# Three row tiles for every expert, and ten looked-up slots for the fourth ones

## The chip, the cores and the metric

The kernel runs on one core of one Trainium2 chip. The metric is the device time of one execution in microseconds (us), and it is compared by the median of several runs. One profiled execution gives the trace: for each engine, when every instruction started, how long it took and what ended the wait in front of it. TensorE (PE) multiplies, VectorE (DVE) and ScalarE (ACT) work element by element, GpSimd (POOL) does small work and starts indirect DMAs, and SyncE (SP) starts ordinary DMAs; ACT starts some too.

## The reference

x has 3125 rows of 256 numbers. Four blocks follow each other, each added to x after a layer norm: three layers of graph attention, a mixture of 16 experts, a sum over graph neighbours, and a mixture of 8 experts. The change touches the second block, which computes, for every row:

```python
probs = softmax(x @ gate_w + gate_b)                 # 16 experts
top_probs, top_idx = top_k(probs, 2)                 # each row goes to two experts
top_probs = top_probs / sum(top_probs)
hidden = silu(x @ w1[e]) * (x @ w2[e])               # 256 -> 512, for each expert e
out = sum over the two experts of  top_prob * (hidden @ w3[e])    # 512 -> 256
```

All of it is in f32. For the inputs that are timed, the 6250 pairs of row and expert spread over the experts as 473, 306, 378, 384, 428, 407, 354, 351, 470, 372, 338, 459, 390, 379, 405 and 356 rows.

## The kernel before

The kernel works on 25 tiles of 128 rows. While the third attention layer is still multiplying, a router handles its output in groups of two tiles (class `Router`): it forms the gate's logits, takes the two best experts of each row, counts with small matmuls how many rows each expert has so far, and writes each normalised row, with its number and its weight, by an indirect DMA into a list in memory, `rows0`. Each expert owns a stretch of 3200 places there (NP), and its rows stand at the beginning of its stretch. An earlier step (`spare_rows`, L1411) has filled the first 512 places (CAP0) of every stretch with spare rows, whose number points behind the real rows and whose weight is zero. The router's last step, `finish` (L660), takes the largest of the sixteen counts. If it is above 512, the flag sends the whole computation to a slower general path at the end (L1516 to L1522); otherwise that path is skipped.

`routed_experts` (L667) then multiplies. For each expert it loads w1, w2 and w3 (512 KB each, ACT's queue, L682 to L686, two buffers), and the first 512 rows of the list as four tiles (`xs`, SP's queue, L688). VectorE copies the rows' numbers to integers (`who`, L690). TensorE transposes the rows (L695) and ScalarE copies them out (L696). For each of the four column blocks of the hidden layer, TensorE forms two products of 128 x 512 (p1 and p2, L703), ScalarE takes silu of the one (L706), and VectorE multiplies it with the other (`hid`, L707). Then, for each of the four row tiles, TensorE multiplies back to 256 columns (L711), VectorE scales by the row's weight (`y`, L714), and POOL starts an indirect DMA that adds the 128 rows of y into `sums` in memory (L716). The accumulates of one expert are independent of each other, since its rows are of different tokens (`independent`, L542); those of the next expert may hold the same tokens and wait for the last expert's to have landed. At the end, five loads bring `sums` back as the new x (L720), and the third block starts from them.

The order on each engine is set by a scheduler that takes program order and available buffers into account: it moves loads and the copy of `who` ahead, so that `who` of the next expert stands in VectorE's queue before the `hid` products of this one. Buffers are recycled: a tile of a pool with two buffers waits until all that used the tile before the last one is done, and for `who` that includes the accumulates which read it.

The last block, `routed_top1` (L723), already works with slots: a table of expert and place for each slot is made on the chip, and SP and TensorE read it into registers (L867, L869) to load rows by a computed address.

Of the kernel before, what the change touches and what calls it, by code (L numbers as in the profile page):

```python
# [9 lines left out]
F32 = mybir.dt.float32  # L10
F16 = mybir.dt.float16
BF16 = mybir.dt.bfloat16
I32 = mybir.dt.int32
U8 = mybir.dt.uint8
F32R = mybir.dt.float32r
AF = mybir.ActivationFunctionType
OP = mybir.AluOpType
AX = mybir.AxisListType
# [3 lines left out]
P = 128  # L22
N = 3125
NT = 25
LAST = N - (NT - 1) * P
NP = NT * P
D = 256
# [492 lines left out]
CAP0 = 512  # L520
CAP1 = 1024
# [26 lines left out]
class Router:  # L548
# [6 lines left out]
    def __init__(self, tc, cp, ident, eps, iota, count, rows, sums, gate_w, gate_b):  # L555
        nc = self.nc = tc.nc
        self.tc, self.ident, self.eps, self.iota, self.rows, self.sums = tc, ident, eps, iota, rows, sums
# [102 lines left out]
    def finish(self, pp, over):  # L660

        total = pp.tile([1, NX0], F32, name="ps_z")
        self.nc.tensor.matmul(total, self.every[:, 0:1], self.pre[:, NT], start=True, stop=True)
        self.nc.vector.tensor_reduce(over, total, AX.X, OP.max)


def routed_experts(tc, x, ident, rows, sums, w1, w2, w3):  # L667
# [6 lines left out]
    nq = CAP0 // P  # L674
    with tc.tile_pool(name="rw", bufs=2) as ep, tc.tile_pool(name="rx", bufs=2) as xp, \
         tc.tile_pool(name="rs", bufs=3) as sp, \
# [3 lines left out]
        for e in range(NX0):  # L680
# [7 lines left out]
            nc.sync.dma_start(xs, rows[e * NP:e * NP + CAP0].rearrange("(q p) f -> p q f", p=P))  # L688
            who = xp.tile([P, nq], I32, name="who")
            nc.vector.tensor_copy(who, xs[:, :, D])  # L690
            xsT = xp.tile([P, KD, CAP0], F32, name="xsT")
            for k in range(KD):
                ps = tp.tile([P, CAP0], F32, name="ps_x")
                for q in range(nq):
                    nc.tensor.transpose(ps[:, q * P:(q + 1) * P], xs[:, q, k * P:(k + 1) * P], ident)  # L695
                nc.scalar.copy(xsT[:, k], ps)  # L696
            hid = xp.tile([P, nh, CAP0], F32, name="hid")
            for j in range(nh):
                p1 = pp.tile([P, CAP0], F32, name="ps_h1")
                p2 = pp.tile([P, CAP0], F32, name="ps_h2")  # L700
                for ps, w in ((p1, a), (p2, b)):
                    for k in range(KD):
                        nc.tensor.matmul(ps, w[:, k, j * P:(j + 1) * P], xsT[:, k], start=(k == 0),  # L703
                                         stop=(k == KD - 1))
                s = sp.tile([P, CAP0], F32, name="silu")
                nc.scalar.activation(s, p1, AF.Silu)  # L706
                nc.vector.tensor_tensor(hid[:, j], s, p2, op=OP.mult)  # L707
            for q in range(nq):
                ps = po.tile([P, D], F32, name="ps_o")
                for j in range(nh):  # L710
                    nc.tensor.matmul(ps, hid[:, j, q * P:(q + 1) * P], o[:, j], start=(j == 0),  # L711
                                     stop=(j == nh - 1))
                y = sp.tile([P, D], F32, name="y")
# [4 lines left out]
                    in_=y, in_offset=None, bounds_check=NP + CAP0 - 1, oob_is_err=True, compute_op=OP.add))  # L718
        for t in range(0, NT, 5):
            nc.sync.dma_start(x[:, t:t + 5], sums[t * P:(t + 5) * P].rearrange("(t p) f -> p t f", p=P))  # L720
# [236 lines left out]
def dense_attention(tc, dram, counts, x_in, big, ident, eps, layers, src, dst, rows, high, make_router, over):  # L957
# [10 lines left out]
    with tc.tile_pool(name="dw", bufs=1) as cp, tc.tile_pool(name="dwl", bufs=2) as wl, \  # L968
# [9 lines left out]
        with tc.tile_pool(name="dp", bufs=8) as pmp, tc.tile_pool(name="ds", bufs=2) as sp, \  # L978
# [148 lines left out]
            router.finish(zp, over)  # L1127
# [283 lines left out]
def spare_rows(tc, cp, rows0, rows1):  # L1411
# [16 lines left out]
    to.append((rows1[NX1 * NP:], empty1))  # L1428
    return [lambda o=o, i=i: nc.scalar.dma_start(o, i) for o, i in to], [empty0[:, 0, 0:1], empty1[:, 0:1]]
# [3 lines left out]
def routed(ctx: ExitStack, tc: tile.TileContext, i: dict, out: bass.AP, over):  # L1433
# [5 lines left out]
    rows0 = dram.tile([NX0 * NP, ROW0], F32, name="rows0")  # L1439
# [4 lines left out]
    early = ctx.enter_context(tc.tile_pool(name="early", bufs=1))  # L1444
    with tc.tile_pool(name="counts", bufs=1) as kp:
# [3 lines left out]
                                                            i["L0_ffn_gate_w"], i["L0_ffn_gate_b"]), over[:, 0:1])  # L1449
        with tc.tile_pool(name="s0", bufs=1) as sp:  # L1450
            ws, wm = (two_halves(nc, sp, i["L1_gnn_" + n], "s_" + n) for n in "WM")
            hidden = hidden_weights(nc, early, *(i["L1_ffn_" + n] for n in ("W1", "b1", "Wg", "bg")), x[:, 0, 0:1])
            routed_experts(tc, x, ident, rows0, sums, *(i["L0_ffn_" + n] for n in ("w1", "w2", "w3")))
# [95 lines left out]
```

## Time and profile before

| quantity | value |
|---|---|
| median of 3 runs | 2082.47 us (2082.14 to 2083.78) |
| the profiled execution's own time | 2082.07 us |
| its span, first to last instruction | 2080.4 us |
| TensorE busy over the span | 1915.8 us, 92% |
| mean granted TensorE clock | 0.982 |
| VectorE, ScalarE, POOL busy | 1010.3, 740.7, 289.3 us |
| attention products (L1075), busy | 864.3 us |
| expert products p1 and p2 (L703), busy | 225.0 us |
| expert output products (L711), busy | 113.1 us |
| accumulates into sums (L716), on POOL | 64, 1552 ns each |
| loads of w1, w2, w3 | 48 of 512 KB, 4.2 us median to landing |
| loads of xs | 16 of 516 KB, 5.8 us median to landing |

The page divides the span into 40 slices of 52 us and gives each engine's busy share in tenths; the experts lie in slices 23 to 29, from 1189.7 us (the first transposes) to 1548.7 us (the last accumulate landed). A group's line gives line, engine, operation, output and inputs, shapes and count, then total busy time, mean duration in ns, and the idle time before it with what ended it. Ends of matmuls are modelled, so durations of single matmuls overlap; rates are better read from start to start. PEld is the load of weights into TensorE.

### The profile page before, as it was taken

How to read it: one execution, taken by the hardware profiler on the slowest of the kernel's cores; microseconds unless marked ns; L12 is line 12 of the kernel's file. 1: busy time of each engine (PE TensorE's matmuls, PEld its weight loads, DVE VectorE, ACT ScalarE, POOL GpSimd, SP SyncE). 2: the span in 40 equal slices, each digit the busy share in tenths (PEclk: the TensorE clock that was granted, in tenths of full speed). 3: DMA queues.
4: the chain of work that ended last, by engine and by line, in shares of the span. 5: the costliest groups of instructions: out<-in, count | busy, mean ns of one | idle time of the engine just before them, and what ended most of it. 6: DMA issues, size and time to landing. Idle time of an engine off the chain costs nothing. (4 is left out here: it accounts for less than half of the span.)

```text
span 2080.4 us, 27180 instructions
## 1 busy us (share of the span) xinstructions
PE 1915.8 (92%) x9234; PEld 1466.8 (71%) x9234; DVE 1010.3 (49%) x2897; ACT 740.7 (36%) x2224; POOL 289.3 (14%) x394
## 2 busy tenths in 40 slices
PE   2999998789999999999999699999979999997986
PEld 2788886668788888788888356556547887555775
DVE  5888886767455544477777422122225222232211
ACT  2866754556010000121111211111116998443221
POOL 1200000000000000023332222323220000222211
PEclk9999999999999999999999799999989999998999
DMA  4002146550000000011111344545530000624553
GB/s 123 25 1 83 42 170 277 203 203 24 3 1 1 0 1 3 8 54 52 49 42 37 122 101 124 130 102 126 127 84 1 1 1 23 240 102 173 190 181 114
DMA packets 97344, 173.82 MB, mean 84 GB/s; under 512 B 9718, under 2 KB 70485, under 8 KB 97168
## 3 DMA queue, kind: packets, MB, share of 16 engines
q10 hardware_dynamic: 37906, 78.75, 10.8%
q1 hardware_dynamic: 42028, 57.91, 8.9%
q0 software_dynamic: 17264, 35.33, 6.5%
q8 instruction: 76, 1.25, 0.2%
q14 instruction: 70, 0.57, 0.1%
HBM read 82.98 MB, written 91.35 MB: 84 GB/s over the span
## 5 line engine op out<-in xcount | busy, mean ns | idle before, releaser
L1075 PE MATMUL acc<-big,pm 128*128 128x257 f32 (+1 forms) x3750 | 864.3, 383 | 2.3 <-DVE pm L1072 2.0
L1075 PEld LDWEIGHTS acc<-big,pm 128*128 128x128 f32 (+1 forms) x3750 | 688.5, 188 | 112.7 <-DVE pm L1072 6.7
L1072 DVE SCALAR_TENSOR_TENSOR pm<-tau,rho,counts 128x256 f32<-128x256 f32 (+1 forms) x975 | 427.0, 467 | 151.7 <-PE acc L1075 150.2
L703 PE MATMUL ps_h<-xsT,w 128*128 128x512 f32 x512 | 225.0, 597 | 3.6 <-ACT xsT L696 3.6
L703 PEld LDWEIGHTS ps_h<-xsT,w 128*128 128x128 f32 x512 | 96.4, 191 | 122.8 <-issue 110.5
L1404 PE MATMUL acc_c<-ohk,ohs 128*128 128x200 f16 x1176 | 135.0, 254 | 31.6 <-ACT ohs L1389 19.7
L1392 DVE TENSOR_TENSOR ohk<-iota_k,key 128x1200 f16<-128x1200 f16 x196 | 151.2, 776 | 20.2 <-PE acc_c L1404 19.4
L1193 PE MATMUL acc<-msg,cr 128*128 128x512 f32 (+1 forms) x625 | 158.0, 405 | 0.1
L1404 PEld LDWEIGHTS <-ohs 128*128 128x128 f16 x1176 | 102.8, 99 | 62.1 <-ACT ohs L1389 32.3
L1407 ACT CAST counts<-acc_c 128x400 uint8<-128x400 f32 x196 | 95.4, 489 | 135.7 <-PE acc_c L1404 131.2
L1189 ACT ACTIVATE cr<-counts 128x256 fp32r<-128x256 uint8 (+1 forms) x325 | 130.6, 402 | 22.0 <-DMA sums<-y,who 13.0
L716 POOL DMA_INDIRECT sums<-y,who x64 | 99.3, 1552 | 265.6 <-DVE y L714 250.9
L1193 PEld LDWEIGHTS acc<-msg,cr 128*128 128x128 f32 (+1 forms) x625 | 115.1, 186 | 28.8 <-ACT cr L1189 1.2
L1388 ACT ACTIVATE far<-iota_s,low 128x128 f16<-128x128 f16 x360 | 124.6, 404 | 4.7 <-issue 2.2
L855 PE MATMUL ps_y<-t_wd,hsT 128*128 x512 | 116.9, 382 | 0.0
L711 PE MATMUL ps_o<-w,hid 128*128 128x256 f32 x512 | 113.1, 379 | 0.0
L711 PEld LDWEIGHTS ps_o<-w,hid 128*128 128x128 f32 x512 | 97.3, 190 | 20.1 <-issue 7.7
L855 PEld LDWEIGHTS ps_y<-t_wd,hsT 128*128 128x128 f32 x512 | 95.5, 192 | 12.0 <-ACT hsT L882 0.3
L706 ACT ACTIVATE silu<-ps_h 128x512 f32<-128x512 f32 x64 | 38.2, 597 | 161.0 <-PE ps_h L703 161.0
L707 DVE TENSOR_TENSOR hid<-silu,ps_h 128x512 f32<-128x512 f32 x64 | 43.7, 687 | 106.4 <-PE ps_h L703 106.3
L764 PE MATMUL ps_H<-big,t_w 128*128 128x512 f32 (+1 forms) x224 | 93.1, 552 | 0.7 <-ACT H L766 0.5
L1094 DVE TENSOR_SCALAR col<-acc 128x2 f32<-128x2 f32 (+1 forms) x39 | 6.1, 156 | 161.1 <-PE acc L1075 161.1
(240 smaller groups left out, 1777.8 us busy)
## 6 DMA issues: line engine op xcount, KB each, us to landing
rows<-empty ACTq DMA_DIRECT2D x16, 2564.0 KB, 8.8
w<-in_L_ffn_w_dram ACTq DMA_DIRECT2D x48, 512.0 KB, 4.2
hs<-rows SPq DMA_DIRECT2D x32, 641.0 KB, 4.1
rows<-empty ACTq DMA_DIRECT2D x16, 516.0 KB, 3.7
xs<-rows SPq DMA_DIRECT2D x16, 516.0 KB, 5.8
t_wd<-in_L_ffn_Wd_dram SPq DMA_DIRECT2D x8, 1024.0 KB, 10.4
bias<-in_L_ffn_bd_dram SPq DMA_DIRECT2D x32, 128.0 KB, 4.0
big<-sums SPq DMA_DIRECT2D x5, 640.0 KB, 8.5
```

Of the source, the lines that this page charges most:

```text
L703: nc.tensor.matmul(ps, w[:, k, j * P:(j + 1) * P], xsT[:, k], start=(k == 0), stop=(k == KD - 1))
L711: nc.tensor.matmul(ps, hid[:, j, q * P:(q + 1) * P], o[:, j], start=(j == 0), stop=(j == nh - 1))
L716: independent(tc, f"sums{e}", nc.gpsimd.indirect_dma_start(out=sums[:, :], out_offset=bass.IndirectOffsetOnAxis(ap=who[:, q:q + 1], axis=0 ...
L855: nc.tensor.matmul(ps, hsT[:, j], d[:, ds(e, 1), j, :].rearrange("p o f -> p (o f)"), start=(j == 0), stop=(j == nh - 1))
L1072: nc.vector.scalar_tensor_tensor(pm[:, :n], tau[:, :n], now.rho[:, s:s + 1], edges[:, s, :n], op0=OP.max, op1=OP.mult)
L1075: nc.tensor.matmul(acc[:r, j, :D + 1], pm[:, q:q + r], now.h[:, s], start=(s == 0), stop=(s == NT - 1))
L1189: nc.scalar.activation(cr[:, :n], edges[:, s, :n], AF.Copy, accum_out=seen[:, a * NT + s:a * NT + s + 1])
L1193: nc.tensor.matmul(acc[:r, j].rearrange("p h d -> p (h d)"), cr[:, q:q + r], msg[:, s].rearrange("p h d -> p (h d)"), start=(s == 0), stop ...
L1388: nc.scalar.activation(far[:, i], self.iota_s, AF.Abs, scale=-1.0, bias=self.low32[:, pair, i:i + 1])
L1392: nc.vector.tensor_tensor(to[:, i:].rearrange("p t (x u) -> p t x u", u=2), iota.rearrange("p (x u) -> p x u", u=2)[:, None].to_broadcast( ...
L1404: nc.tensor.matmul(acc[:, u], ohs[:, i], ohk[:, i], start=(t == 0), stop=(t == TW - 1))
L1407: nc.scalar.copy(to[:, :, d0 % PAIR:d0 % PAIR + 2 * WIN].rearrange("p s (u d) -> p u s d", u=2), acc.rearrange("p u (s d) -> p u s d", d=WIN))
```

## The change

Every expert now multiplies three tiles (EACH = 3), so 384 rows. For experts with more than 384 rows, ten slots (MORE = 10) follow, each of one tile. `finish` makes the table of slots on the chip: it compares each count with 384, forms running sums over the experts, and finds for each slot which expert is its, and so where the fourth tile begins. Slots that are left over take the last expert's weights and a spare tile behind the lists, which `spare_rows` now fills too. If more than ten experts have a fourth tile, the flag is set that sends the work to the general path.

In a slot, SP reads the expert and the place into registers and loads the tile and the three weights by computed addresses. TensorE transposes two blocks, forms p1 and p2 as 16 products of 128 columns into one bank each, ScalarE and VectorE take silu and product in two halves, TensorE multiplies back with four products, VectorE scales, and POOL starts one accumulate, which is a group of its own. The weights' pool has three buffers instead of two, silu's two instead of three, and y has a pool of three.

```diff
+EACH = 3
+MORE = 10
...
-    def finish(self, pp, over):
-
+    def finish(self, cp, pp, over):
+        nc = self.nc
         total = pp.tile([1, NX0], F32, name="ps_z")
+        nc.tensor.matmul(total, self.every[:, 0:1], self.pre[:, NT], start=True, stop=True)
+        nc.vector.tensor_reduce(over, total, AX.X, OP.max)
+        end = cp.tile([1, 5, 2 * NX0], F32, name="more_end")
+        nc.vector.memset(end, 0.0)
+        nc.vector.tensor_scalar(end[:, 0, NX0:], total, float(EACH * P), None, op0=OP.is_gt)
+        for j in range(4):
+            nc.vector.tensor_tensor(end[:, j + 1, NX0:], end[:, j, NX0:], end[:, j, NX0 - (1 << j):-(1 << j)],
+                                    op=OP.add)
+        end = end[:, 4, NX0:]
+        much = cp.tile([1, 1], F32, name="more_much")
+        nc.vector.tensor_scalar(much, end[:, NX0 - 1:], float(MORE), float(2 * CAP0), op0=OP.is_gt, op1=OP.mult)
+        nc.vector.tensor_tensor(over, over, much, op=OP.max)
+        slot = cp.tile([1, MORE], F32, name="more_slot")
+        nc.gpsimd.iota(slot, pattern=[[1, MORE]], base=0, channel_multiplier=0, allow_small_or_imprecise_dtypes=True)
+        done = cp.tile([1, MORE, NX0], F32, name="more_done")
+        nc.vector.tensor_tensor(done, end[:, None, :].to_broadcast([1, MORE, NX0]),
+                                slot[:, :, None].to_broadcast([1, MORE, NX0]), op=OP.is_le)
+        nc.vector.tensor_reduce(slot, done, AX.X, OP.add)
+        table = self.table
+        nc.vector.tensor_scalar(table[:, 0], slot, float(NX0 - 1), None, op0=OP.min)
+        nc.vector.tensor_scalar(slot, slot, float(NP), float(EACH * P), op0=OP.mult, op1=OP.add)
+        nc.vector.tensor_scalar(table[:, 1], slot, float(NX0 * NP), None, op0=OP.min)
...
-    nq = CAP0 // P
-    with tc.tile_pool(name="rw", bufs=2) as ep, tc.tile_pool(name="rx", bufs=2) as xp, \
-         tc.tile_pool(name="rs", bufs=3) as sp, \
+    nq = EACH
+    with tc.tile_pool(name="rw", bufs=3) as ep, tc.tile_pool(name="rx", bufs=2) as xp, \
+         tc.tile_pool(name="rs", bufs=2) as sp, tc.tile_pool(name="ry", bufs=3) as yp, \
...
-            nc.sync.dma_start(xs, rows[e * NP:e * NP + CAP0].rearrange("(q p) f -> p q f", p=P))
+            nc.sync.dma_start(xs, rows[e * NP:e * NP + EACH * P].rearrange("(q p) f -> p q f", p=P))
...
+        for slot in range(MORE):
+            e = nc.values_load(table[0:1, 0, slot:slot + 1], engines=(mybir.EngineType.SP,), min_val=0,
+                               max_val=NX0 - 1, skip_runtime_bounds_check_because="min with the last expert")
+            at = nc.values_load(table[0:1, 1, slot:slot + 1], engines=(mybir.EngineType.SP,), min_val=0,
+                                max_val=NX0 * NP, skip_runtime_bounds_check_because="min with the spare tile")
+            xs = xp.tile([P, ROW0], F32, name="xs")
+            nc.sync.dma_start(xs, rows[ds(at, P)])
+            a = ep.tile([P, KD, HID0], F32, name="w1")
+            nc.sync.dma_start(a, w1[ds(e, 1)].rearrange("o (k p) h -> p (o k) h", p=P))
+            b = ep.tile([P, KD, HID0], F32, name="w2")
+            nc.sync.dma_start(b, w2[ds(e, 1)].rearrange("o (k p) h -> p (o k) h", p=P))
+            o = ep.tile([P, nh, D], F32, name="w3")
+            nc.sync.dma_start(o, w3[ds(e, 1)].rearrange("o (k p) f -> p (o k) f", p=P))
+            who = xp.tile([P, 1], I32, name="who")
+            nc.vector.tensor_copy(who, xs[:, D:D + 1])
+            xsT = xp.tile([P, KD, P], F32, name="xsT")
+            ps = tp.tile([P, KD, P], F32, name="ps_x")
+            for k in range(KD):
+                nc.tensor.transpose(ps[:, k], xs[:, k * P:(k + 1) * P], ident)
+            nc.scalar.copy(xsT, ps)
+            p1 = pp.tile([P, nh, P], F32, name="ps_h1")
+            p2 = pp.tile([P, nh, P], F32, name="ps_h2")
+            for ps, w in ((p1, a), (p2, b)):
+                for j in range(nh):
+                    for k in range(KD):
+                        nc.tensor.matmul(ps[:, j], w[:, k, j * P:(j + 1) * P], xsT[:, k], start=(k == 0),
+                                         stop=(k == KD - 1))
+            hid = xp.tile([P, nh, P], F32, name="hid")
+            for j in range(0, nh, 2):
+                s = sp.tile([P, 2, P], F32, name="silu")
+                nc.scalar.activation(s, p1[:, j:j + 2], AF.Silu)
+                nc.vector.tensor_tensor(hid[:, j:j + 2], s, p2[:, j:j + 2], op=OP.mult)
+            ps = po.tile([P, D], F32, name="ps_o")
+            for j in range(nh):
+                nc.tensor.matmul(ps, hid[:, j], o[:, j], start=(j == 0), stop=(j == nh - 1))
+            y = yp.tile([P, D], F32, name="y")
+            nc.vector.tensor_scalar(y, ps, xs[:, D + 1:D + 2], None, op0=OP.mult)
+            independent(tc, f"more{slot}", nc.gpsimd.indirect_dma_start(
+                out=sums[:, :], out_offset=bass.IndirectOffsetOnAxis(ap=who, axis=0), in_=y, in_offset=None,
+                bounds_check=NP + CAP0 - 1, oob_is_err=True, compute_op=OP.add))
...
+    to.append((rows0[NX0 * NP:], empty0[:, 0]))
...
-    rows0 = dram.tile([NX0 * NP, ROW0], F32, name="rows0")
+    rows0 = dram.tile([NX0 * NP + P, ROW0], F32, name="rows0")
...
+    more = early.tile([1, 2, MORE], I32, name="more")
```

In the expert loop every CAP0 in a tile's width becomes EACH * P, and `y` comes from its own pool.

## The prediction

> **What bounds the kernel now.** I read the page's slices first, then the groups, the waits of the expert stage (1190 to 1549 us) and one expert's timeline.
>
> ```profile
> PE   2999998789999999999999699999979999997986
> PEclk9999999999999999999999799999989999998999
> ...
> L703 PE MATMUL ps_h<-xsT,w 128*128 128x512 f32 x512 | 225.0, 597 | 3.6 <-ACT xsT L696 3.6
> ...
> L711 PE MATMUL ps_o<-w,hid 128*128 128x256 f32 x512 | 113.1, 379 | 0.0
> ```
> TensorE is 9 tenths busy at full clock through the slices of the expert stage (23 to 29), so its passes set the pace there. An f32 matmul is two passes, hence x512 for 256 matmuls. One expert as a timeline (start, length, engine):
>
> ```profile
> 1492.67 7.07 PE L711 MATMUL ps_o<-w,hid 128*128 128x256 f32 x32
> ...
> 1499.07 1.55 POOL L716 DMA_INDIRECT sums<-y,who  x1 [0.30 <-issue]
> ...
> 1499.58 1.04 PE L695 MATMUL ps_x<-ident,xs 128*128 128x128 f32 x8
> 1499.78 0.38 ACTq L686 DMA_DIRECT2D w<-in_L_ffn_w_dram  x1
> 1499.78 0.48 DVE L714 TENSOR_SCALAR y<-ps_o,xs 128x256 f32<-128x256 f32 x1 [1.25 <-PE ps_o L711]
> ...
> 1500.29 0.36 SPq L688 DMA_DIRECT2D xs<-rows  x1
> 1500.85 14.00 PE L703 MATMUL ps_h<-xsT,w 128*128 128x512 f32 x32 [0.24 <-ACT xsT L696]
> 1500.92 1.55 POOL L716 DMA_INDIRECT sums<-y,who  x1 [0.30 <-issue]
> ...
> 1506.76 0.17 DVE L690 CAST who<-xs 128x4 int32<-128x4 f32 x1 [6.50 <-DMA sums<-y,who]
> 1506.87 0.69 DVE L707 TENSOR_TENSOR hid<-silu,ps_h 128x512 f32<-128x512 f32 x1
> ...
> 1514.69 1.67 PE L711 MATMUL ps_o<-w,hid 128*128 128x256 f32 x7
> ```
> The cycle is 22.02 us (L703 starts at 1500.85, one expert before at 1478.83): 13.84 for the 32 passes of L703 (to the start of L711, 1478.83 to 1492.67), 6.91 for the 32 passes of L711 (1492.67 to 1499.58), 1.27 for eight transposes and the first copy (1499.58 to 1500.85). T below is 1499.58, where an expert's last output matmul ends. Beside this runs a second chain that hides: the four accumulates leave POOL 1.86 apart, the last at T+1.34, and VectorE's copy of `who` (L690), which belongs to the next expert, waits until that last one has landed, with the `hid` product queued behind it.
>
> ```profile
> DVE who L690 <- DMA sums<-y,who: 96.1, 14, 8.0
> ```
> Columns: total, times, longest. Nobody waits for VectorE in turn, since TensorE needs that p2 bank back only at T+9.9 (1.27 + 5 x 1.73). How long a landing takes depends on its company (issues of one accumulate each, start in us):
>
> ```profile
> L716 POOL DMA_INDIRECT sums<-y,who x1: 1551/1551/1551, 1499.1 to 1499.1; - x1
> ...
> DMA to landing us min/median/max: 5.8/5.8/5.8
> ```
> ```profile
> L716 POOL DMA_INDIRECT sums<-y,who x1: 1551/1551/1551, 1545.0 to 1545.0; - x1
> ...
> DMA to landing us min/median/max: 3.7/3.7/3.7
> ```
> 5.8 us while w3 (issued at 1499.78) and xs (1500.29) come in, 3.7 us at the end, when nothing is being loaded. The fourth of this group took 5.8 too; over fourteen groups, from the last accumulate's start to `who`, the mean is 6.16, 5.76 to 7.3.
>
> **Experts with three tiles: -88.2 us.** Passes cost by their columns: 0.4325 us at 512 (13.84/32), 0.216 at 256, so 0.324 at 384. L703 becomes 10.38, L711 loses a quarter of its passes, 5.18, transposes and copy 0.95: 16.51 instead of 22.02. Sixteen times 5.51 is 88.2.
>
> **The copy of `who` now bites: +7.** In the changed kernel as built it still stands ahead of the first `hid` product. The last accumulate leaves at T+1.2 (three at POOL's spacing); the gap to `who` I take as 5.8 (6.16 less 0.37, the missing 129 KB of xs at 350 GB/s); `who` to the end of the product was 0.80, now 0.63; to TensorE 0.24: T+7.87. TensorE wants that p2 bank back for its third column block, after 0.95 + 5 x 1.30 = T+7.43. So 0.44 us, fifteen times (experts 1 to 14 and slot 0's copy): 7. Ends: 0 with a gap of 3.7, 29 with 7.3 (1.94 each).
>
> **Ten slots: +90.2.** TensorE alone: a 128-column pass is (1.16-0.28)/7 = 0.126 us in
>
> ```profile
> 1892.31 1.16 PE L764 MATMUL ps_H<-big,t_w 128*128 128x128 f32 x8
> ```
> so 32 passes 4.0 (4.3 with their tail), two transposes 0.3, eight passes of L711's size 1.72: 6.2 per slot. But every slot is its own group, and in the built order the copy of `who` for slot s+1 stands before slot s's `hid` products. It reuses the buffer that slot s-1's accumulate reads, so slot s cannot form `hid`, nor run its output matmuls, before that accumulate has landed. From end of y to end of y: POOL 0.28, start to `who` 5.84 (as 1500.92 to 1506.76), `who` and a 256-column product 0.53, to TensorE 0.24, output matmuls 1.72, to y 0.21, y 0.48: 9.30. The first is 0.26 longer, eight are 9.30, the tenth has no copy behind it and takes TensorE's 6.2: 90.2. The landing is the unknown: loads in company at these offsets (w1 0.7 us after the accumulate's start, w2 1.2) resemble the 5.8 row (w3 0.7 after, xs 1.2 after), which I take. Ends 3.7 (-18.9 in nine periods) and 7.2, the longest of the page's 64 (+12.6).
>
> [...]
>
> **What hides in a slot.** SP: two register loads and four DMAs per slot, behind the wait for y of slot s-1. xs leaves 0.13 later, the weights by about 2.6 (0.83 between SP issues in the last stage, register loads included). 1.65 MB at
>
> ```profile
> 1780.00:1784.00 4.00, 4.00 (x31) 2.70 (x24) 2.58 (x11) 0.59 (x1) 0.00 (x0) 1.00 1.10 350
> ```
> 350 GB/s (last column) is 4.7 us, so all land by about 8.5 after y(s-1); w1 is needed 0.7 us before y(s), at 8.6, the others later. Hidden by little: loads 1 us later than this and paced the same would be met by w1 alone, 1 us a slot. xs, 2.3 us for 128 KB, is there in time for its transposes. big<-sums, queued behind them on SP, waits for the last accumulate anyway.
>
> **The ends: +1.7.** `finish` puts about twelve one-partition VectorE operations at 0.15 to 0.35 us among the last router group's; ten lie ahead of the last g_wt, which POOL's last two row sends wait for, and the first xs waits for these: +2.1 (ends 0 and 3). The third weight buffer loads 1.5 MB more in that idle stretch, behind the other two: 0, at worst 2. The single extra fill joins 33 on ACT's queue in the first attention layer, and POOL's iota an idle POOL: 0; if their cover went, under 1 us together. At the far end the last accumulate starts 0.28 after y instead of 0.66: -0.4. Small reorderings in the early stages: 0, plus or minus 3. POOL's six accumulates fewer and the shorter silu and `hid` operations were not on the path: 0.
>
> **Sum.** -88.2 + 7 + 90.2 + 1.7 = +10.7. The profiled execution took 2082.07 (span 2080.4), 0.4 under the median 2082.47: 2082.47 + 10.7 = 2093.
>
> **Rivals.**
> *The accumulates land early.* For it: 3.7 in the last group, and the slot's own xs is only 129 KB. Against: an accumulate that starts 0.7 us before a load already took 5.8. At 3.7 the slots cost 71.3 and the sum is -8.2: 2074, faster. It turns at a landing of 4.6 (10.7/9 below 5.8), and it is faster beyond 0.2% below about 4.15.
>
> *The clock drops in the slots.* TensorE idles 9.3 - 6.2 = 3.1 us a slot. The granted clock after the stage's end (the last three columns are clock, DMA share, GB/s):
>
> ```profile
> 1546.00:1548.00 2.00, 0.00 (x0) 0.00 (x0) 0.00 (x0) 0.00 (x0) 0.51 (x1) 1.00 0.67 87
> 1548.00:1550.00 2.00, 0.00 (x0) 0.00 (x0) 0.06 (x1) 1.21 (x6) 0.00 (x0) 0.65 0.23 26
> ```
> The last matmul ended near 1543.8; full clock held to about 1548.8, 5 us, then half. A 3.1 us gap is shorter, which speaks against it; its recurring speaks for it. At half clock the output matmuls take 3.45, and nine slots 15.5 more: 2108. [...]
>
> *It doesn't do what it says.* More than ten experts above 384 rows would send everything to the general path, whose time no row shows. From the reference's inputs seven are above 384, the most 473: under 1 in 100. Three slots then multiply the spare tile at full price.
>
> **How the numbers follow.** My forecast (landing 4.9 to 6.5, clock full, 2085 to 2105) 0.50; clock 0.20; early landings 0.17; the rest, longer stalls or late weights, 0.13, mostly above 2100. Early landing reaches down to 2070 with the experts' stall gone as well (-7 more would be 2067, left out); the clock with 7.2 landings reaches 2121 (2093 + 15.5 + 12.6). Range 2070 to 2120. What a measurement here can tell from no change is 0.2%, 4.2 us: faster (below 2078.3) 0.17, same 0.14, slower 0.69.
>
> **What would show it.** Expert cycles of 16.5 to 17.5 us; VectorE's `who` waiting for sums DMAs in nine slots, with TensorE idle before the output matmuls; y to y near 9.3; the clock in the slots; the first xs about 2 us later. The forecast is wrong if slot accumulates land under 4.6 us, if the pace is set by a weight load, or if the clock falls.

## The result, and the profile after

The changed kernel takes 2114.1 us (median of four runs, 2108.7 to 2119.0), the kernel before 2082.6 us beside it: a ratio of 1.0147, with a 95% interval of 1.0126 to 1.0168. It is 31.5 us slower, where 10.7 us had been forecast. The direction and the range held (2070 to 2120), the size did not.

Two rows of the page of the changed kernel, its 40 slices with TensorE's busy share and granted clock in tenths:

```profile
PE   2999998789999999999999599998659999997986
PEclk9999999999999999999999799999779999999999
```

The slots run from 1464 to 1578 us, which is slices 27 (its last third) to 29. TensorE falls from 9 tenths to 8, 6 and 5 there, and the clock to 7 in two slices. In the kernel before, the clock showed 8 in one slice there, after the last expert.

One slot of the changed kernel as a timeline (start, length, engine, line, operation, and in brackets the idle time before it with what ended it):

```profile
1486.53 4.10 PE L772 MATMUL ps_h<-xsT,w 128*128 128x128 f32 x32
...
1486.77 0.48 DVE L783 TENSOR_SCALAR y<-ps_o,xs 128x256 f32<-128x256 f32 x1 [3.10 <-PE ps_o L781]
1487.29 0.35 SPq L753 DMA_DIRECT2D xs<-rows  x1
1487.54 1.55 POOL L784 DMA_INDIRECT sums<-y,who  x1 [9.91 <-DVE y L783]
1488.13 0.37 SPq L755 DMA_DIRECT2D w<-in_L_ffn_w_dram  x1
1488.73 0.37 SPq L757 DMA_DIRECT2D w<-in_L_ffn_w_dram  x1
...
1489.68 0.38 SPq L759 DMA_DIRECT2D w<-in_L_ffn_w_dram  x1
...
1493.82 0.15 DVE L761 CAST who<-xs 128x1 int32<-128x1 f32 x1 [6.56 <-DMA sums<-y,who]
1493.92 0.75 DVE L778 TENSOR_TENSOR hid<-silu,ps_h 128x256 f32<-128x256 f32 x2
...
1494.40 3.52 PE L781 MATMUL ps_o<-w,hid 128*128 128x256 f32 x8 [3.55 <-DVE hid L778]
...
1497.96 0.48 DVE L783 TENSOR_SCALAR y<-ps_o,xs 128x256 f32<-128x256 f32 x1 [3.29 <-PE ps_o L781]
```

The chain is the one forecast: the accumulate starts 0.29 us after y ends, the copy of `who` (L761) waits for it to land, the `hid` product stands behind that copy on VectorE, and the eight passes of the output matmuls wait for `hid`. Two lengths differ. From the accumulate's start to `who` it takes 6.28 us here, forecast 5.84. And the eight passes are shown with 3.52 us, after a gap of 3.55 us in which TensorE had nothing to do. Over the ten slots, the instructions of the accumulate's line and its time to landing:

```profile
L784 POOL DMA_INDIRECT sums<-y,who x10: 1549/1549/1549, 1476.1 to 1578.6; - x10
...
DMA to landing us min/median/max: 3.5/6.6/8.5
```

The output matmuls of the slots, and the clock in two microseconds of them (the last three columns are granted clock, DMA share, GB/s):

```profile
L781 PE MATMUL ps_o<-w,hid x80: 379/634/794, 1472.5 to 1577.4; 128*128 128x256 f32 x80
```

```profile
1484.00:1486.00 2.00, 2.00 (x6) 1.64 (x5) 0.00 (x0) 0.00 (x0) 0.00 (x0) 0.50 0.00 0
```

A median of 634 ns for a pass that takes 379 ns in the experts, and a clock of 0.50. The waits (total, times, longest):

```profile
DVE who L761 <- DMA sums<-y,who: 72.4, 10, 8.8
...
PE ps_o L781 <- DVE hid L778: 36.5, 10, 5.1
```

The first is the copy of `who`, in all ten slots; the second is TensorE, which waits for what stands behind that copy.

The experts behave as forecast. In the profile they end (y of the last tile) at 1464.32 us instead of 1544.30, 80.0 us earlier. The ten slots then take 114.0 us to the last y. A second profile of the changed kernel, whose execution took 2114.1 us and so lies at the median, has the experts' end at 1462.92, the slots at 109.6 us and 539.9 us from the last y to the end of the span.

### The profile page after: what moved, and what is told of

Its sections match the earlier page's. It is cut to its first block, busy times and chain, and to the rows that moved or that the text cites. A ratio compares the mean times of both kernels' runs of the same rounds, so it can differ in the third digit from the quotient of the medians.

```text
span 2117.2 us, 27956 instructions
## 1 busy us (share of the span) xinstructions
PE 1908.5 (90%) x9494; PEld 1506.1 (71%) x9494; DVE 1008.3 (48%) x2934; ACT 739.7 (35%) x2254; POOL 281.1 (13%) x389
## 3 DMA queue, kind: packets, MB, share of 16 engines
q10 hardware_dynamic: 38050, 78.88, 10.6%
## 5 line engine op out<-in xcount | busy, mean ns | idle before, releaser
L731 PE MATMUL ps_h<-xsT,w 128*128 128x384 f32 x512 | 172.1, 494 | 5.7 <-ACT xsT L724 4.7
L1472 PE MATMUL acc_c<-ohk,ohs 128*128 128x200 f16 x1176 | 134.7, 253 | 31.5 <-ACT ohs L1457 18.7
L744 POOL DMA_INDIRECT sums<-y,who x48 | 74.5, 1552 | 208.6 <-DVE y L742 173.3
L739 PE MATMUL ps_o<-w,hid 128*128 128x256 f32 x384 | 85.5, 379 | 0.0
L1015 PE MATMUL ps_m<-we,yT 128*128 128x258 f32 x300 | 80.4, 397 | 3.9 <-ACT big L1022 2.3
L739 PEld LDWEIGHTS ps_o<-w,hid 128*128 128x128 f32 x384 | 73.0, 190 | 13.3
L1460 DVE TENSOR_TENSOR ohs<-iota_s,low 128x512 f16<-128x512 f16 (+1 forms) x196 | 82.0, 427 | 0.0
## 6 DMA issues: line engine op xcount, KB each, us to landing
rows<-empty ACTq DMA_DIRECT2D x16, 2564.0 KB, 10.6
```

What stands on the lines that cost most here:

```text
L1460: nc.vector.tensor_tensor(to[:, i:].rearrange("p t (x u) -> p t x u", u=2), iota.rearrange("p (x u) -> p x u", u=2)[:, None].to_broadcast( ...
L1472: nc.tensor.matmul(acc[:, u], ohs[:, i], ohk[:, i], start=(t == 0), stop=(t == TW - 1))
```

## The experiments

The theory: each slot is paced by one chain, accumulate, landing, `who`, `hid`, output matmuls; it is longer than forecast because the accumulate lands later among the slot's own weight loads (6.6 us in the median), and because TensorE's clock falls to 0.50 in or shortly after the gap that this leaves on it (3.4 to 5.1 us in the first profile). All ratios are to the kernel before, run beside each experiment, whose medians there were 2082.7 to 2087.5 us. "Period" is the mean time from one slot's y to the next in the trace, nine intervals, 11.39 us in the changed kernel's first profile and 10.81 in its second. The first slot is not in it.

**The list gets its own buffers.** This takes away what makes the copy of `who` wait, a buffer that the accumulate of two tiles before still reads.

```diff
+         tc.tile_pool(name="rwho", bufs=4) as wp, \
-            who = xp.tile([P, nq], I32, name="who")
+            who = wp.tile([P, nq], I32, name="who")
-            who = xp.tile([P, 1], I32, name="who")
+            who = wp.tile([P, 1], I32, name="who")
```

> The destination list `who` gets a pool of its own with four buffers, in the experts and in the slots; nothing else differs from the changed kernel (2114 us, ten slots 114.0 us, 11.4 us each). Theory A (the copy of the list waits for the accumulate of two tiles before, holds VectorE, and so holds the hidden product and the output matmuls): the copy waits no more, a slot falls to the time that one accumulate takes from its issue to its landing under the weight loads, 6.7 to 7.2 us, since the next accumulate into the same rows starts only after it; ten slots 68 to 75 us, the experts lose about 3.6 us as well, time 2065 to 2075 us, below the kernel before (2082.5). Rival B (the slots are paced by their weight loads, 1.5 MB each, whatever VectorE waits for): the copies wait for xs instead, a slot stays at 10.5 us or above, time 2100 to 2114. Rival C (the half clock of the output matmuls is a cause of its own and stays): 1.7 us a slot is left on top, 8.4 to 9 us a slot, 2083 to 2090.

Measured: 2073.0 us, 0.9932 (0.9913 to 0.9952), faster than before. The period is 6.53 us, and output matmuls take 379 ns a pass in the median. The wait for the accumulates is replaced by one for the load of xs:

```profile
DVE who L762 <- DMA xs<-rows: 32.2, 10, 4.4
```

Theory A holds. The period is a little below what it foretold, since only four of ten accumulates had to wait for the one before them (17.7 us together). Rivals B and C fall: loads of 1.5 MB do not pace a slot at 10 us, and the half clock goes with the gap (at most 0.6 us before the output matmuls here).

**TensorE is kept busy.** Six more matmuls stand ahead of the output matmuls and are overwritten by them.

```diff
             ps = po.tile([P, D], F32, name="ps_o")
+            for j in range(6):
+                nc.tensor.matmul(ps, xsT[:, 0], o[:, j % nh], start=True, stop=True)
             for j in range(nh):
```

> Six extra matmuls per slot, into the bank that the output matmuls overwrite, stand between the hidden layer's matmuls and the output matmuls, where TensorE is idle 3.4 to 4.5 us in each slot; the output is unchanged. Theory A with the clock as second term (the output matmuls take 3.3 to 3.8 us in place of 1.72 because the clock has dropped to half in that gap): they return to about 1.7 to 2.0 us, a slot falls from 11.4 to 9.6 to 10.0 us, time 2097 to 2102. Rival (the output matmuls are slow for another cause, such as late w3 or VectorE's second half of the hidden product): output matmuls stay at 3.3 us or more, and the time is 2114 to 2120. The accumulates' landing (6.7 us) does not change under either.

Measured: 2105.1 us, 1.0085 (1.0069 to 1.0102). More work makes it faster than the changed kernel, by 9 us in the medians and 0.6% in the ratios. The landing stays (6.4 us in the median), the period falls to 10.10 us, and the output matmuls are back:

```profile
L783 PE MATMUL ps_o<-w,hid x80: 379/379/631, 1473.3 to 1565.8; 128*128 128x256 f32 x80
```

So the clock is a term of its own. From the start of `who` to the end of y it takes 3.1 us in eight of nine slots here and 4.5 us on average in the changed kernel's second profile, about 1.3 us a slot. The median time gains less than expected (2097 to 2102), and one slot of the ten still showed 3.01 us for its eight passes, after a gap of 2.00 us, where the other nine showed 1.9 to 2.0.

**The slots load no weights.** They multiply by the weights of expert 15 that are in the buffers, so the products of the fourth tiles are those of the wrong expert.

```diff
-            a = ep.tile([P, KD, HID0], F32, name="w1")
-            nc.sync.dma_start(a, w1[ds(e, 1)].rearrange("o (k p) h -> p (o k) h", p=P))
...
-            nc.sync.dma_start(o, w3[ds(e, 1)].rearrange("o (k p) f -> p (o k) f", p=P))
```

> The slots load no weights and multiply by those of expert 15 that are in the buffers already (the slots' products are left at the wrong weights; all other work is done). Theory A (an accumulate lands late because it shares the DMA engines with the slot's own 1.5 MB of weights): it lands in 3.5 to 3.9 us in place of 6.7, a slot takes 7.2 to 8.9 us (the upper end with the output matmuls still at half clock), time 2073 to 2089. Rival (the landing is the accumulate's own cost, or the slots' chain has another link): landing stays above 5.5 us, slots at 10 us or more, time 2100 to 2114.

Measured: 2075.5 us, 0.9940 (0.9923 to 0.9958). The landing:

```profile
DMA to landing us min/median/max: 3.6/3.8/3.8
```

The period is 7.08 us, the eight output passes take 1.99 us in every slot, after gaps of 0.6 to 1.5 us, although the copy of `who` still waits for the accumulates (41.9 us over ten slots). Without the slot's own loads the landing is 3.8 us instead of 6.6.

**Rows of 1 KB in the loads.** Beside the loads the accumulate lands 2.8 us later than without them (6.6 against 3.8 us). If this delay goes with the length of the loads' rows, half the length leaves half of it, a landing of about 5.2 us (an estimate from these two landings); if it does not, the landing stays at 6.6.

```diff
-            nc.sync.dma_start(a, w1[ds(e, 1)].rearrange("o (k p) h -> p (o k) h", p=P))
+            for c in range(0, HID0, D):
+                nc.sync.dma_start(a[:, :, c:c + D], w1[ds(e, 1), :, c:c + D].rearrange("o (k p) h -> p (o k) h", p=P))
(b and w2 likewise)
```

> The slots' w1 and w2 are loaded in two column halves each, so that their rows are 1 KB, as long as the accumulate's, in place of 2 KB; bytes and order unchanged, two DMA issues more per slot. [...]

Measured: 2095.8 us, 1.0057 (1.0039 to 1.0074), landing 5.2 us, period 8.85 us. Seen alone, this fits a delay that goes with the length of the rows, to the number. With rows of 512 B (four column quarters of w1 and of w2) a quarter of it would be left, a landing of 4.5 us by the same estimate:

> The changed kernel with w1 and w2 of the slots in four column quarters each, rows of 512 B. Landing was 3.7 us without loads, 5.2 us with rows of 1 KB, 6.6 us with 2 KB. [...]

Measured: 2087.8 us, 1.0006 (0.9995 to 1.0016), landing 4.5 us (by the time to `who`, since the trace has the landing of three of the ten accumulates only), period 8.06 us. That fits too. The clock still fell in three slots, after gaps of 1.7 to 1.9 us: their eight output passes took 2.7 to 3.7 us, in the others 1.9 to 2.0. But both kernels also issue more and smaller DMAs, so a control was needed that splits the loads and leaves the rows at 2 KB.

**The control: as many DMAs, rows as they were.**

```diff
-            nc.sync.dma_start(a, w1[ds(e, 1)].rearrange("o (k p) h -> p (o k) h", p=P))
+            for k in range(KD):
+                nc.sync.dma_start(a[:, k:k + 1], w1[ds(e, 1), k * P:(k + 1) * P].rearrange("o p h -> p o h"))
(b and w2 likewise)
```

> The changed kernel with w1 and w2 of the slots loaded in two halves each, but split by the blocks of 128 input rows, so that the rows stay 2 KB long; number of DMA issues and bytes of each are those of the variant with rows of 1 KB (2095.8 us, landing 5.2 us, 8.85 us a slot). If the length of the rows sets how long an accumulate lands: landing 6.4 to 6.8 us as in the changed kernel, a slot 11 to 11.6 us, time 2110 to 2120. If it was the number or the pace of the issues: landing about 5.2 us, a slot about 8.9 us, time about 2096.

Measured: 2097.9 us, 1.0060 (1.0043 to 1.0077). The landing of the control, with rows of 2 KB:

```profile
DMA to landing us min/median/max: 3.6/5.0/5.4
```

The expectation by the length of rows falls, and with it the reading of the two runs above: the number or the pace of the issues went with the difference (5.0 us here and 5.2 with rows of 1 KB, against 6.6). The period of the control is 9.46 us and not 8.9, since the clock fell in eight of its slots (2.7 to 3.7 us for the eight output passes, 2.0 in the others), against five with rows of 1 KB (2.5 to 3.8 us).

**The loads leave later.** xs is loaded in two, or four, column pieces; this pushes the weights back on SP's queue and leaves their DMAs as they were.

```diff
-            nc.sync.dma_start(xs, rows[ds(at, P)])
+            for c0, c1 in ((0, 64), (64, 128), (128, 192), (192, 258)):
+                nc.sync.dma_start(xs[:, c0:c1], rows[ds(at, P), c0:c1])
(in two pieces: ((0, 128), (128, 258)))
```

> The changed kernel with a slot's xs loaded in two column pieces; weights, their DMAs and rows as they were, but each issued about 0.5 us later, so that one of them (512 KB) and no longer two (1 MB) is issued before POOL has finished the accumulate's issue, 1.55 us after its start. If the accumulate lands behind what was issued before it (512 KB at 350 GB/s is 1.5 us, on 3.7 us alone): landing about 5.2 us, a slot 8.8 to 9.6 us, time 2095 to 2101. If the size of a single DMA counts (an accumulate takes turns with whole DMAs of 512 KB): landing 6.4 to 6.8, time 2109 to 2117.

> The same with xs in four pieces, weights issued about 1.5 us later than in the changed kernel, all of them after POOL's issue of the accumulate. If it lands behind what was issued before it: landing 3.7 to 4.2 us, a slot 7.2 to 7.8 us with full clock, time 2079 to 2086. If the size of a single DMA or the mere overlap with 1.5 MB of loads counts: landing 5 us or more, time 2096 or more. If the weights now come too late, p1 waits for w1 and a slot takes 8 us or more at a short landing.

In two pieces: 2095.3 us, 1.0051 (1.0033 to 1.0070), period 9.25 us. Time and period are those forecast for an accumulate that lands behind what was issued before it; the landing was to be 5.2 us and has no single value. The trace has the landing of three accumulates only, so the time to `who` less 0.1 us stands for it: 5.6 to 5.9 us in six of the nine cases, where w1 left 1.0 to 1.3 us after the accumulate's start, 4.3 where it left at 1.50, and 3.7 where it left at 1.79. One case does not fit: 7.2 us with w1 at 1.15. The slot with 3.7 us has the order of the changed kernel on VectorE and all three weights:

```profile
1491.11 1.55 POOL L785 DMA_INDIRECT sums<-y,who  x1 [6.88 <-DVE y L784]
1492.90 0.38 SPq L756 DMA_DIRECT2D w<-in_L_ffn_w_dram  x1
...
1494.86 0.15 DVE L762 CAST who<-xs 128x1 int32<-128x1 f32 x1 [4.02 <-DMA sums<-y,who]
1494.96 0.75 DVE L779 TENSOR_TENSOR hid<-silu,ps_h 128x256 f32<-128x256 f32 x2
```

From y to y that slot takes 7.12 us, with 1.99 us for its eight output passes. The kernel before shows the same: the accumulate that starts at 1497.21, one before the row that the prediction used, has w3 and xs issued 2.57 and 3.08 us after its start (1499.78 and 1500.29), and lands as if alone:

```profile
L716 POOL DMA_INDIRECT sums<-y,who x1: 1552/1552/1552, 1497.2 to 1497.2; - x1
...
DMA to landing us min/median/max: 3.8/3.8/3.8
```

In four pieces: 2073.1 us, 0.9954 (0.9939 to 0.9970), better than expected and faster than the kernel before, with all weights loaded. One slot of it:

```profile
1491.15 1.95 SPq L754 DMA_DIRECT2D xs<-rows  x4
1491.40 1.55 POOL L785 DMA_INDIRECT sums<-y,who  x1 [5.54 <-DVE y L784]
...
1493.61 0.38 SPq L756 DMA_DIRECT2D w<-in_L_ffn_w_dram  x1
...
1495.38 0.75 DVE L779 TENSOR_TENSOR hid<-silu,ps_h 128x256 f32<-128x256 f32 x2 [4.26 <-PE ps_h L773]
...
1495.86 1.99 PE L782 MATMUL ps_o<-w,hid 128*128 128x256 f32 x8 [0.41 <-DVE hid L779]
1496.51 0.15 DVE L762 CAST who<-xs 128x1 int32<-128x1 f32 x1 [0.38 <-DMA xs<-rows]
```

w1 leaves 2.21 us after the accumulate's start. But a second thing differs in this run: `hid` (1495.38) now stands before the copy of `who` (1496.51) on VectorE, in all slots but the first and the last, which has no copy behind it; in the changed kernel and with two pieces the copy comes first. With that order nothing that TensorE needs stands behind the copy, whatever the landing, and the copy waits for an accumulate once in the slots (4.5 us). The 41 us that this run gains over the changed kernel can therefore not be put down to the later loads alone; how much each of the two brought was not separated. The landings, of the three accumulates for which the trace has one:

```profile
DMA to landing us min/median/max: 3.7/3.8/4.0
```

Two of the three have the weights in company, issued from 2.21 and 2.89 us on (4.0 and 3.7 us); the third has no load beside it (3.8). In the first slot, with w1 at 1.97, the time to `who` gives 3.9. The size of a single DMA is excluded by the run with two pieces, since its weights are still three DMAs of 512 KB and land the accumulate in 5.7, 4.3 or 3.7 us instead of 6.4 to 6.8. What all these runs have in common is how much had been issued early. The offsets are from the start of the accumulate, the bytes are those of the weight loads issued in the first 1.8 us after it (its issue on POOL ends at 1.55):

| kernel | weight DMAs issued at | issued by 1.8 us | landing |
|---|---|---|---|
| changed kernel | 0.60, 1.16, 1.78 | 1.5 MB | 6.6 |
| kernel before, the row used (w3 and xs) | 0.71, 1.22 | 1.0 MB | 5.8 |
| xs in two, most slots | 1.15, 1.72, 2.35 | 1.0 MB | 5.7 |
| rows of 1 KB | 0.6, 1.2, 1.7 and later, 256 KB each | 0.75 MB | 5.2 |
| control, rows of 2 KB | 0.6, 1.1, 1.6 and later, 256 KB each | 0.75 MB | 5.0 |
| rows of 512 B | 0.6, 1.2, 1.7 and later, 128 KB each | 0.38 MB | 4.5 |
| xs in two, one slot | 1.50, 2.07, 2.71 | 0.5 MB | 4.3 |
| xs in two, another slot | 1.79, 2.35, 3.03 | 0.5 MB | 3.7 |
| xs in four, three slots | 1.97 to 2.89 and later | 0 | 3.7 to 4.0 |
| kernel before, one accumulate ahead (w3 and xs) | 2.57, 3.08 | 0 | 3.8 |
| slots without weight loads | none | 0 | 3.8 |

About 3.8 us and 2 us more for each MB describes the rows to within 0.3 us, but for the two single slots of "xs in two", which are 0.5 and 1.1 us lower. It is a description, and its limit of 1.8 us was set after the runs; the forecast had gone by 1.55 us, the end of POOL's issue. Two slots do not fit it at all (8.5 us in the changed kernel's first profile, and the 7.2 us above), and one accumulate was late with loads that had been issued shortly before its start and were still under way: that at 1500.92 in the kernel before, with w3 and xs issued 1.14 and 0.63 us ahead of it and landing 4.2 and 5.7 us after their issue, took 5.8 us. The cutoff is not sharp either: in two slots of the changed kernel's profiles w3 left at 2.14 instead of 1.78, and `who` came after 6.0 and 6.3 us, in a third w3 left at 1.86, and `who` came after 5.8, where most others have 6.4 to 6.9. The trace shows 1.55 us for the accumulate's instruction on POOL and 3.8 us to its landing alone; a w3 issued at 1.78 us, after that instruction's end, is among the loads of the slots with 6.6 us. That the accumulate queues behind these loads was not shown.

**The slots left out.** The rows of the fourth tiles are missing from the output.

```diff
-        for slot in range(MORE):
+        for slot in range(0):
```

> The ten slots are left out (the rows of the fourth tiles are missing from the output); router, table, experts with three tiles and the later blocks stay. The prediction's terms without the slots: -88.2 + 7 + 1.7 = -79.5 us against the kernel before, so 2003 to 2006 us; by the changed kernel's trace (the experts end 80.0 us earlier) the same. If the later blocks are themselves slower than before (their stretch after the last landing was 2.6 to 5.2 us longer in the profiles of the changed kernel and its variants), 2006 to 2011 us, and that excess is no matter of the slots.

Measured: 2009.0 us, 0.9634 (0.9619 to 0.9649), 78.5 us below the median of the kernel before beside it (2087.5). The forecast for this part was 79.5. The experts' last y ends at 1464.32 us, as in the changed kernel. From there to the end it is 542.3 us, where the kernel before has 536.1 and 537.9; what the later blocks add is taken up below.

**Further along the chain.** With the list's own buffers, the load of xs is next. Here three slots share one of the buffers of xs; in the second run w1 and w2 also come in column halves; in the third the list has ten buffers instead of four besides.

```diff
-            xs = xp.tile([P, ROW0], F32, name="xs")
+            if slot % nq == 0:
+                trio = xp.tile([P, nq, ROW0], F32, name="xs")
+            xs = trio[:, slot % nq]
...
-          tc.tile_pool(name="rwho", bufs=4) as wp, \
+          tc.tile_pool(name="rwho", bufs=10) as wp, \
```

> On top of the list's own buffers (2073 us, 6.5 us a slot, where the list now waits for the load of xs, 32 us over ten slots) three slots share one of the buffers of xs, so that a slot's rows are loaded earlier. Theory A (after the list, the late xs is next in the chain): a slot falls to TensorE's own 6.0 to 6.2 us, time 2068 to 2071. Rival (the accumulates, one after another at 6.7 us under denser loads, or the weight loads of 1.5 MB a slot set the pace): slots at 6.5 us or more, time 2072 to 2078.

> The variant with early xs and own list buffers, and w1 and w2 loaded in column halves with rows of 1 KB. If the order of the accumulates sets the pace in the former, its landing falls to about 5.2 us and the slots to 6.0 to 6.2 us: 2066 to 2071 us. If the loads of the weights set it, more and shorter packets make it no better: 2071 to 2078 us.

> The fastest variant so far (2067.5 us) with ten buffers for the list instead of four: in its trace the list of a slot is copied further ahead and still waited for accumulates, 33 us over seven copies, which cost the first slots 5 us (the first y ends 7.4 us after the last of the experts, with half clock in its output matmuls). Theory: those waits go, the first slots fall to 6.1 us, time 2061 to 2065. Rival: the copies now wait for something else at the same place (the loads of the first slots, issued while the last experts' rows still arrive), time 2066 to 2069.

Measured: 2069.5 us, 0.9923 (0.9909 to 0.9937); 2067.5 us, 0.9912 (0.9898 to 0.9927); and 2066.0 us, 0.9910 (0.9890 to 0.9930). The periods are 6.03, 6.02 and 5.78 us. They leave the first slot out, which takes 12.1, 11.2 and 8.4 us here against 7.1 with the list's own buffers alone, and the ten slots together take 66.3, 65.3 and 60.4 us against 65.8. So the earlier xs shortened later slots and lengthened the first. Alone it made neither the ratio (0.9923 against 0.9932) nor the sum clearly better, and that the late xs was next in the chain is not shown. In all three `hid` also stands before `who` on VectorE from the second slot on. The third run has the lowest time, but the ratio of the second, and at 2066.0 us it lies at the lower edge of its rival's range, so it does not decide between the two; its slots are 5 us shorter in the trace, while the stretch behind them is 6 us longer (544.1 against 538.2). Its two halves of the slots, with busy time of PE, PEld, DVE, ACT and POOL, then clock, DMA share and GB/s:

```profile
1466.00:1496.00 30.00, 28.47 (x210) 26.58 (x209) 6.88 (x20) 4.59 (x14) 6.20 (x4) 1.00 1.01 295
1496.00:1524.00 28.00, 25.52 (x182) 23.28 (x180) 6.48 (x18) 4.97 (x17) 7.75 (x5) 1.00 0.59 158
```

TensorE is 9 tenths busy at full clock: these slots are bound by their matmuls, but for the accumulates, which wait for one another and of which the last leaves POOL 3.2 us after the last y (0.3 in the changed kernel). What remains of the gain against the kernel before is small, about 19 us, since the ten slots take back 60 of the 80.

**Both kernels once more.** In the first profile of the kernel before, the last block's products took 160.6 us from first to last, in the changed kernel 164.6.

> The kernel before, profiled once more. In its first profile the last block's products (ps_y, first to last) took 160.6 us; in the changed kernel and eight variants 162.3 to 166.0 us. If that is a lasting difference, it takes 160.0 to 161.5 us here; if it is spread from one execution to the next, 162 us or more.

> The changed kernel, profiled once more. The last block's products: 162.3 to 166.0 us by the variants. The slots: 11.2 to 11.6 us each, with output matmuls at half clock in eight or nine of ten, landings 6.5 to 6.8 us.

Measured: 162.3 us in the kernel before, 165.0 in the changed one, whose slots had landings of 6.5 us in the median, took 10.0 to 11.9 us each (the first 12.3, the last 6.9) and showed the lower clock in nine of ten (2.6 to 3.8 us for the eight output passes, 1.99 in the tenth). The kernel before lies at 160.6 and 162.3, the changed kernel and all its variants at 162.2 to 166.4. By the bound set beforehand this is spread between executions, though narrowly; a remainder of 2 or 3 us in a block that the change does not touch is not excluded, and its cause is open.

## Why the prediction was right or wrong

**Experts, -88.2, and the copy of `who`, +7: right in their sum, by luck.** With the +2.1 of `finish` they give -79.1 at the experts' last y, and the two profiles have -80.0 and -81.6. Term by term it is different. The steady cycle is 16.8 us, forecast 16.51 and 0.44 for the stall. With the list's own buffers, where no copy in the experts waits for an accumulate, the cycle is 16.74 us as well. So the stall cost 0.04 to 0.1 us a time in the two profiles, about 1 us in all instead of 7, and the cycle without it is 0.23 longer than forecast, nearly 4 us over sixteen. The two errors go against each other. The +2.1 is not settled: the first transposes start at 1191.78 against 1189.70 us in the first profiles and at 1188.83 against 1189.06 in the second, and over all runs of the changed kernel and its variants at 1187.7 to 1191.9.

**Ten slots, +90.2: wrong by 19 to 24 us, and this is nearly the whole miss.** The chain was right, and so was its working where it can be tested: 0.28 to POOL, the landing, and 3.18 from `who` to the end of y. Put the measured time to `who` in place of 5.84 and the formula gives 8.0 us for 4.57 (rows of 512 B, where four slots at full clock took 7.6 to 8.0) and 7.3 for 3.8 (no loads, 7.1 to 7.3 measured). With a busy TensorE it gives 10.2 for 6.76, the mean of its eight full periods, and 10.26 was measured. Two terms of it were mis-sized. The profile at the median time shows 11.30 us in the eight full periods, 2.0 above the 9.30:

- The step that failed first is the landing, "loads in company at these offsets (w1 0.7 us after the accumulate's start, w2 1.2) resemble the 5.8 row". From start to `who` it took 6.52 us on average there, so +0.68. The row had 1 MB at these two offsets and no more. The slot has a third load, w3, 0.6 us behind w2, which was not counted. The table above points to that load; no run took it alone away, so that part stays argued.
- The step that failed with the larger price is "A 3.1 us gap is shorter, which speaks against it". Start of `who` to the end of y took 4.50 us instead of 3.18, so +1.32: in nine of ten slots the eight output passes took 2.6 to 3.8 us, where they take 1.99 at full clock; in the first profile, with 2.7 to 3.8 us, the trace shows a clock of 0.50 over all of them or over a part. The gaps in those nine were 2.7 to 4.4 us. The two terms are not independent: with landings of 3.8 us (no loads) the gaps were 0.9 to 1.5 us in nine slots, with 5.2 us (rows of 1 KB) 1.6 to 3.1, and there half of the ten slots kept their clock.

Eight periods give 16 us, the first slot 12.27 instead of 9.56 (+2.7), the last 6.91 instead of 6.2 (+0.7): 19.4 us.

**The rivals.** "The clock drops in the slots", at 0.20, is what happened, and its +15.5 for nine slots was nearly the price (1.32 x 8 is 10.6, and the first slot). Seen from the runs it should have been the forecast even with a landing of 5.84: the gap was put at 3.1 us, and in the slots of all runs gaps of 2.9 us and above cost clock every time (2.5 to 3.8 us for the eight passes). It was counted with the forecast landing, though a late landing and a lost clock come together; that pair was kept for the end of the range (2121). "The accumulates land early" was wrong for this kernel, but its price was right: without the loads the landing was 3.8 us, the ten slots took 71.3 us (given for 3.7: 71.3), and the time was 2075.5 against the 2074 given. "It doesn't do what it says" played no part.

**The clock and the delay.** Gaps of 2.9 to 5.1 us before the output matmuls all cost clock here, those of 2.0 to 2.9 did in some slots and not in others, and most below 1.9 did not. In the changed kernel's first trace the granted clock is at 0.50 in the slots for 3.4 or 6.8 us at a time (1473.6 to 1477.1, 1504.4 to 1511.2). What sets the moment of its fall was not shown. The clock after the experts, which the prediction read as held for 5 us, held for 4.8 us there (to 1548.60) and said little about shorter gaps that come again and again. The delay was 2.1 us (5.8 less 3.7) in the row that the prediction used, where two loads on two queues (SP's and ACT's) stood beside the accumulate; in the slots, with three loads on SP's alone, it was 2.9 (6.6 less 3.7). The control showed that the length of the loads' rows is not what sets it (5.0 us with rows of 2 KB, 5.2 with 1 KB).

**The ends, +1.7: not settled.** From the last y to the end it is 538.9 and 539.9 us in the changed kernel's two profiles, 536.1 and 537.9 in those of the kernel before, so about +2.4 where -0.4 was forecast. Some of it is in the last block, and its cause is open. The +2.1 at the experts' start is not settled, as said above.

Sum, at the median profile and against the mean of the two profiles of before: experts' end -81.6 (1462.92 against 1544.30 and 1544.82), slots +109.6, rest +2.9, together +30.9, against 31.5 measured.

## What to carry to other kernels

When a small instruction (here a 0.15 us copy of row numbers) reuses a buffer that a DMA still reads, look at what stands behind it on its engine: four tiny buffers were worth 41 us here, more than the whole loss. Look at the order on that engine again when a variant comes out better than its theory allows: with xs in four pieces the order had changed along with the loads. When a landing time is taken from a row of the profile, compare all that is issued around it, also what comes after the part that resembles, since a third load went with 0.7 us more a period here. And a chain that leaves TensorE idle for 3 us a period is better priced at both clocks, together with whatever lengthens the gap: here a pass behind such gaps took 634 ns in the median and 379 without them.

## What was not expected of the hardware

- An accumulate of 128 rows landed after 3.8, 4.5, 5.2, 5.8 or 6.6 us in most cases as 0, 0.38, 0.75, 1.0 or 1.5 MB of loads had been issued in its first 1.8 us. Loads issued 2.2 us or more after its start did not delay it (3.7 to 4.0 us in three cases).
- Rows of 1 KB and of 2 KB in the loads made no clear difference to the landing at the same number of DMAs (5.2 and 5.0 us, with 2095.8 and 2097.9 us in time).
- Six useless matmuls a slot made the kernel 9 us faster (2105.1 against 2114.1 us): the gaps before the output matmuls were 2.0 us at most instead of 3.4 to 5.1, and a pass took 379 ns in the median instead of 634.
